# Second layer's local attention: the first pass by 64 queries and 192 keys, and TensorE tiles of 32 rows by 64 columns for both passes

## The chip, the core and the metric

The kernel runs on one core of a Trainium2 chip. The metric is the device time of one execution in microseconds; the time before is 2541.93 us, the median of three runs (2540.92, 2541.93, 2542.63). Engines are named as in the profile: PE (TensorE matmul), PEld (TensorE weight load), DVE (VectorE), ACT (ScalarE), POOL (GpSimd), SP (SyncE, whose queue issues most DMAs). L665 is line 665 of the kernel before.

## The reference, cut to what matters

Two layers run over x of shape (2, 2048, 256), in float32. Each layer normalises x, computes an attention s and a gate g, and adds s * g to x. The change is in the attention of the second layer alone. It has 16 heads of 16 channels, and a query sees the keys at most 64 positions away:

```python
def _local_mask(seq_len):
    idx = jnp.arange(seq_len)
    band = jnp.abs(idx[:, None] - idx[None, :]) <= WINDOW // 2     # WINDOW = 128
    return jnp.where(band, 0.0, -jnp.inf).astype(jnp.float32)
...
scores = jnp.einsum('bhqd,bhkd->bhqk', q, k) * SCALE + mask
attn = jax.nn.softmax(scores, axis=-1)
out = jnp.einsum('bhqk,bhkd->bhqd', attn, v)
out = out.transpose(0, 2, 1, 3).reshape(b, s, D)
return out @ w_out + b_out
```

The first layer has the same shape of attention without a mask, then a feed-forward part with low-rank experts; the second layer's feed-forward part is a linear layer with eight gated low-rank experts.

## The kernel before

**Stages.** The program is unrolled and runs: weights and first norm, the first layer's feed-forward part, its attention (about 1100 to 2125 us), the second norm with the second layer's feed-forward part and its first q and k (2125 to 2290 us), the second layer's attention (2290 to 2505 us), and a tail. One function, `attention`, serves both layers; `local=True` is the second layer.

**Layout.** Heads go in groups of four (`NG`). A group's q and k lie as [128, tokens] tiles: each head has 32 rows (`HP`), of which 16 are channels; of the other 16, k holds ones, and q holds the negated maximum of the query in the first and zeros in the rest. So a score is a matmul with 32 rows of contraction, and the four heads of a group lie on the four row groups of PE's array. `hp[j]` is the row slice of head j. In the local case k has 64 columns of padding (`PAD`) on either side.

**Items and steps.** An item is one batch element, one group of heads, and a block of 512 queries: 2 x 4 x 4 = 32 items. In the local case an item has two steps (`U` = 2), each over 256 queries, two tiles of 128. So there are 64 steps. In step s the loop calls, in this order: `scores(second, first, es)`, where `second` is step s and `first` is step s + 5 (`U + LEAD`); `weigh` for the step two back (`DEL`); and whatever `after` holds for the step.

**First pass** (in `scores`, L652 to L665): it finds each query's largest score. For each head and each of the two query tiles, one matmul takes 128 queries as the stationary operand and up to 256 keys as the moving one (`reach`, L691, cuts 64 columns off at a sequence's ends), and writes `sq`, which has a bank for each head of a pair. The pairs are (2, 3) and (0, 1); there are two `sq` buffers of two banks. DVE then adds the mask, a [128, 256] band that is the same for every tile, and takes the maximum along the keys (L672, output `seen` and a column of `mx`).

**Maximum** (`place_max`, L704 to L710): after every second step, PE transposes `mx` of a coming item into `pmx`, ACT negates it into `row`, and a DMA issued by ACT writes it into the extra row of q.

**Second pass** (in `scores`, L618 to L634): scores are computed again, with keys as the stationary operand, into `sk`, one bank per head. A bank has 512 columns: query tile 0 against key tile 0, both query tiles against key tile 1 (256 columns), and query tile 1 against key tile 2. So three matmuls per head, of 256, 128 and 128 columns, listed in `segs`. ACT takes the exponential of each bank (L681); POOL zeroes what lies outside the band, two selects for each pair of heads (L686).

**Weighing** (`weigh`, L721 to L736): 12 matmuls per step with v as the stationary operand (32 columns per head, so in tiles of 128 rows by 32 columns) accumulate into one bank `acc`; the pieces are 128, 256 and 128 columns. ACT copies 256 columns out to `av`.

**Banks.** `sk`, `acc`, `pmx` and the output projection's `pr` share the tag "m" of a pool of four PSUM banks, which they take in turn.

**Order on PE.** `scores` collects its matmuls as `pieces` with a number `when`, and issues them sorted by it. In a step with both passes (`apart`) the heads 0 and 1 of the second pass go beside the heads 2 and 3 of the first, and then the other way round, so that all four row groups have work:

```python
when = 2 * (j // 2) if apart else 0          # second pass, then += 2 * (hi - lo) / TB
when = (2, 2, 0, 0)[j] if apart else 0       # first pass, + t for the query tile
for _, o, lhs, rhs in sorted(pieces, key=lambda x_: x_[0]):
    nc.tensor.matmul(o, lhs, rhs, start=True, stop=True)
```

Each float32 matmul appears in the records as two passes, each with its own weight load.

**After an item.** The numerators and denominators go out and back by DMA (`away`, `compact`, `write`, `spread`), DVE inverts the denominators, and `divide` multiplies, on DVE and POOL in turn. After the last group of heads two output projections per item follow (L819 to L826). q and k of later groups are fetched in halves by SP.

**The mask** (L554 to L563): DVE fills a [128, 256] tile with zeros and POOL cuts the band with two selects; these instructions stand, on their engines, in the stage of the second norm, near 2133 us.

Of the kernel before, what the change touches and what calls it, by code (L numbers as in the profile page):

```python
# [10 lines left out]
F32 = mybir.dt.float32  # L11
I32 = mybir.dt.int32
AF = mybir.ActivationFunctionType
ALU = mybir.AluOpType
# [3 lines left out]
P = 128  # L18
# [7 lines left out]
TB = 512  # L26
# [4 lines left out]
MASKED = -1e30  # L31
# [6 lines left out]
def two_layers(ctx: ExitStack, tc: tile.TileContext, a, out):  # L38
    nc = tc.nc
# [444 lines left out]
    def attention(A, scale, local, final, start=None, projected=False):  # L484
# [18 lines left out]
        with ExitStack() as st:  # L503
# [43 lines left out]
            hp = [slice(j * HP, (j + 1) * HP) for j in range(NG)]  # L547
            ep = None if local else pool("ep", 8)
# [3 lines left out]
            if local:  # L552

                mask = mp.tile([P, 2 * P], F32, name="mask", bufs=1)  # L554
                nc.vector.memset(mask, 0.0)
                nc.gpsimd.affine_select(
                    out=mask, in_=mask, compare_op=ALU.is_ge, fill=MASKED, base=0,
# [3 lines left out]
                    out=mask, in_=mask, compare_op=ALU.is_ge, fill=MASKED, base=P,  # L561
                    pattern=[[-1, 2 * P]], channel_multiplier=1,
                )  # L563

# [29 lines left out]
            def scores(second, first, es):  # L594
# [7 lines left out]
                if second:  # L602
# [3 lines left out]
                    if local:  # L606

                        qt = n * TT + 2 * u
                        segs = [
                            (P, 3 * P, bass.ts(qt + 1, P), bass.ds(qt * P, 2 * P)),  # L610
                            (0, P, bass.ts(qt, P), bass.ts(qt, P)),
                            (3 * P, 4 * P, bass.ts(qt + 2, P), bass.ts(qt + 1, P)),
                        ]
                    else:
                        segs = [(0, TB, bass.ts(u, P), bass.ts(n, TB))]
# [8 lines left out]
                    for j in range(NG):  # L624
# [6 lines left out]
                        when = 2 * (j // 2) if apart else 0  # L631
                        for lo, hi, ks_, qs_ in segs:
                            pieces.append((when, t[:, lo:hi], k[hp[j], ks_], q[hp[j], qs_]))
                            when += 2 * (hi - lo) / TB  # L634
                        tasks.append((es[j], t))
                pairs = []
                if first:
# [9 lines left out]
                    for pair in ((2, 3), (0, 1)):  # L647
                        sq = pmax.tile([P, 2, TB], F32, name="sq", tag="sq")
                        pairs.append((pair, sq))
                        for d, j in enumerate(pair):  # L650
                            when = (2, 2, 0, 0)[j] if apart else 0
                            if local:  # L652
                                for t in range(2):
                                    qt, lo, hi = reach(n1, u1, t)
                                    pieces.append((
                                        when + t, sq[:, d, t * 2 * P + lo : t * 2 * P + hi],
                                        q1[hp[j], bass.ts(qt, P)], k1[hp[j], qt * P + lo : qt * P + hi],
                                    ))
# [7 lines left out]
                for pair, sq in pairs:  # L666
                    if local:
                        for d, j in enumerate(pair):
                            for t in range(2):
                                qt, lo, hi = reach(n1, u1, t)  # L670
                                seen = mp.tile([P, 2 * P], F32, name="seen", tag="seen")
# [498 lines left out]
```

## Time and profile before

| what | value |
|---|---|
| median of three runs | 2541.93 us (2540.92 to 2542.63) |
| the profiled execution, own time | 2539.57 us |
| its span on the core | 2537.7 us |
| granted PE clock over the span | 0.999 |
| second layer's attention, 2290 to 2505 us: PE, DVE, ACT, POOL busy | 213.2, 182.8, 149.9, 175.1 of 215 us |
| second norm and feed-forward part, 2125 to 2290 us: PE, DVE, ACT, POOL busy | 163.4, 59.3, 57.5, 10.9 of 165 us |
| first layer's attention, 1100 to 2125 us: PE, DVE busy | 1021.8, 804.5 of 1025 us |

The times come from one profiled execution, in which each instruction has a start and a length. The ends of matmuls are modelled, so "busy" on PE is an upper view. In a group's line the first part names line, engine and operation, then output and inputs by the program's names, their shapes and how many there were; behind the bar stand the busy time in us, the mean of one in ns, and the idle time of the engine just before them with what ended it. A timeline line merges neighbouring instructions of the same kind: start, length of the merged piece, and after the x the number of instructions. Matmuls in different tiles of the array overlap, so their lengths don't add up; the distance from start to start tells the pace.

### The profile page before, as it was taken

What the parts mean: (1) busy time and instruction counts of PE and PEld (TensorE: products, weight loads), DVE (VectorE), ACT (ScalarE), POOL (GpSimd) and SP (SyncE); (2) the same over time, 40 slices, a digit from 0 to 9 for tenths busy, and PEclk for the clock granted to TensorE, in tenths of its full rate; (3) what the DMA queues carried; (4) which work ended last, traced back from release to release, by engine and by line L of the source; (5) the groups of instructions that cost most, each with busy time, mean ns of one, the idle gap of its engine ahead of it and who ended that gap; (6) DMA issues with size and microseconds to landing.
All of it is one profiled execution on the core that took longest, in us unless ns stands there. A gap on an engine that the chain in (4) does not pass through costs nothing.

```text
span 2537.7 us, 47965 instructions
## 1 busy us (share of the span) xinstructions
PE 2514.2 (99%) x18928; PEld 1062.5 (42%) x18928; DVE 1686.9 (66%) x2744; ACT 1625.0 (64%) x3190; POOL 879.6 (35%) x830
## 2 busy tenths in 40 slices
PE   8999999999999999999999999999999999999999
PEld 5444444543333333333333333333333334457766
DVE  4143333157888888888777788888888765238986
ACT  5300000127888888888888888888888886227755
POOL 0000000102344444444444444444444430016887
PEclk9999999999999999999999999999999999999999
DMA  6131111330001001001001001001000002133552
GB/s 243 51 88 51 52 51 34 113 86 14 16 12 43 16 12 43 17 12 48 12 12 43 16 13 43 16 12 43 16 12 10 16 12 61 50 133 107 167 161 83
DMA packets 80689, 129.56 MB, mean 51 GB/s; under 512 B 27408, under 2 KB 32400, under 8 KB 77904
## 3 DMA queue, kind: packets, MB, share of 16 engines
q1 hardware_dynamic: 78592, 125.20, 15.7%
q8 instruction: 148, 2.42, 0.4%
q10 hardware_dynamic: 1872, 1.31, 0.2%
q14 instruction: 77, 0.63, 0.1%
HBM read 80.24 MB, written 45.70 MB: 50 GB/s over the span
## 4 chain that ended last, share of the span: by engine, by line
PE 80%; DVE 0%; ACT 0%; issue 0%; POOL 0%; ACTq 0%; POOLq 0%; DVEq 0%
PE sk L665 25%; PE acc L731 23%; PE sq L665 19%; PE pp L477 4%; PE pr L819 2%; PE pp L530 2%; PE po L1007 1%; PE pt L1003 1%; PE po L1015 1%; PE pmx L704 0%; PE xb L138 0%; PE xb L113 0%; DVE part L677 0%; PE of L811 0%; PE pw L990 0%
## 5 line engine op out<-in xcount | busy, mean ns | idle before, releaser
L677 DVE TENSOR_REDUCE part<-sq 128x2 f32<-128x1024 f32 x1024 | 1207.3, 1221 | 301.6 <-PE sq L665 301.2
L681 ACT ACTIVATE e<-sk 128x512 f32<-128x512 f32 x2048 | 1058.3, 603 | 222.7 <-PE sq L665 194.2
L665 PE MATMUL sk<-q,k 32*128 32x512 f32 (+2 forms) x5632 | 1141.6, 533 | 1.4 <-ACT xn L681 1.0
L665 PE MATMUL sq<-k,q 32*128 32x512 f32 (+2 forms) x5120 | 1129.5, 569 | 1.3 <-DVE part L677 1.3
L745 POOL TENSOR_TENSOR av<-av,more 128x512 f32<-128x512 f32 x462 | 585.0, 1266 | 941.1 <-ACT more L744 941.1
L665 PEld LDWEIGHTS sk<-q,k 32*128 32x128 f32 x5632 | 523.2, 184 | 579.8 <-ACT e L681 482.9
L731 PE MATMUL acc<-e,v 128*32 128x512 f32 x4096 | 546.4, 605 | 0.0
L665 PEld LDWEIGHTS sq<-k,q 32*128 32x128 f32 x5120 | 407.5, 183 | 23.7 <-DVE part L677 12.2
L744 ACT COPY more<-acc 128x512 f32<-128x512 f32 x462 | 270.4, 585 | 1.0 <-issue 0.5
L731 PEld LDWEIGHTS acc<-e,v 128*32 128x32 f32 x4096 | 81.5, 108 | 388.3 <-ACT e L681 378.4
L461 ACT ACTIVATE gt<-po 128x512 f32<-128x512 f32 x16 | 8.8, 594 | 321.1 <-PE po L457 321.1
L672 DVE CUSTOM_DVE_ANT_0 seen<-sq,mask 128x256 f32<-128x256 f32 (+1 forms) x512 | 176.2, 410 | 52.7 <-PE sq L665 46.3
L467 POOL TENSOR_TENSOR x<-x,up 128x512 f32<-128x512 f32 x16 | 23.1, 1461 | 446.5 <-DVE up L464 446.5
L448 DVE TENSOR_TENSOR xs<-we,px 128x512 f32<-128x512 f32 x64 | 44.0, 687 | 136.1 <-PE px L440 131.8
L686 POOL TENSOR_SCALAR_AFFINE_SELECT xn<-xn 128x512 f32<-128x512 f32 x172 | 105.9, 649 | 77.8 <-ACT xn L681 74.0
L440 PE MATMUL px<-xn,FV 128*128 128x512 f32 x256 | 121.2, 595 | 0.0
L444 PE MATMUL py<-cum,FW 128*128 128x512 f32 x256 | 120.5, 593 | 0.6 <-DVE cum L412 0.6
L424 PE MATMUL po<-pr,UO 128*128 128x512 f32 x256 | 119.0, 592 | 0.0
L681 ACT ACTIVATE xn<-sk 128x512 f32<-128x512 f32 x172 | 89.9, 601 | 40.6 <-PE sk L665 17.9
L450 DVE TENSOR_TENSOR pr<-xs,py 128x512 f32<-128x512 f32 x64 | 44.0, 688 | 64.9 <-PE py L444 64.6
L424 PEld LDWEIGHTS po<-pr,UO 128*128 128x128 f32 x256 | 48.6, 190 | 61.2 <-issue 61.0
L444 PEld LDWEIGHTS py<-cum,FW 128*128 128x128 f32 x256 | 48.4, 190 | 61.5 <-issue 59.8
(195 smaller groups left out, 1608.0 us busy)
## 6 DMA issues: line engine op xcount, KB each, us to landing
we<-wd SPq DMA_DIRECT2D x128, 128.0 KB
ad<-av SPq DMA_DIRECT2D x59, 256.0 KB
qd<-sb SPq DMA_DIRECT2D x48, 256.0 KB
k<-qd SPq DMA_DIRECT2D x10, 1024.0 KB
q<-qd SPq DMA_DIRECT2D x10, 1024.0 KB
xn<-ad SPq DMA_DIRECT2D x59, 128.0 KB
recb<-rd SPq DMA_DIRECT2D x59, 128.0 KB
q<-qd SPq DMA_DIRECT2D x12, 512.0 KB
```

What stands on the lines that cost most here:

```text
L424: nc.tensor.matmul(po[oc], UO[:, ch, bass.ts(oc, P)], pr, start=(ch == 0), stop=False)
L440: nc.tensor.matmul(px, FV[:, c, bass.ts(ch, P)], xn[b][:, c, cols], start=(c == 0), stop=(c == NC - 1))
L444: nc.tensor.matmul(py, FW[:, c, bass.ts(ch, P)], cum[:, c, :], start=(c == 0), stop=(c == NC - 1))
L477: nc.tensor.matmul(ps, w[:, c, bass.ts(hf, P)], xn[b][:, c, bass.ts(n, TB)], start=(c == 0), stop=(c == NC - 1))
L665: nc.tensor.matmul(o, lhs, rhs, start=True, stop=True)
L672: nc.vector.tensor_tensor_reduce(seen[:, lo:hi], sq[:, d, t * 2 * P + lo : t * 2 * P + hi], mask[:, lo:hi], 1.0, LOWEST, ALU.add, ALU.max, ...
L677: nc.vector.tensor_reduce(pt[:, pair[0] : pair[1] + 1, t, kb], sq, AX.X, ALU.max)
L681: nc.scalar.activation(e, t, AF.Exp, scale=scale)
L686: nc.gpsimd.affine_select(out=e[:, :, c, :], in_=e[:, :, c, :], compare_op=ALU.is_ge, fill=0.0, base=0, pattern=[[0, 4], [sign, P]], chann ...
L731: nc.tensor.matmul(acc[hp[j], o : o + hi - lo], vs[b][:, kt, vcols(g, j)], es[j][:, lo:hi], start=(r == 0), stop=(r == len(parts) - 1), sk ...
L744: nc.scalar.copy(more, acc)
L745: nc.gpsimd.tensor_tensor(avs[i], avs[i], more, ALU.add)
```

## The change

The first pass is cut into tiles of 64 queries, each against the 192 keys that its queries can reach: `RC` is 192, and the two halves of a query tile (`halves`) write partitions 0 to 63 and 64 to 127 of `sq`. Where one matmul had 128 stationary and up to 256 moving columns, two now have 64 and 192 each. The reduction on DVE reads 192 columns instead of 256. Since the two halves start at keys that are 64 apart, the mask is shifted by 64 for the lower half; at a sequence's first and last tile the padding columns are masked, so there are three masks of [128, 192], made of the old band (now `reach`) by six copies and two fills on DVE. The function `reach` is gone.

The second pass keeps its columns, but takes the keys in two halves of 64, each writing its half of the partitions of `sk`. So both passes use tiles of 32 rows and 64 columns. The numbers `when` are set to the new lengths. Per step the first pass issues 16 matmuls instead of 8 and the second 24 instead of 12. The first layer issues what it did before.

```diff
--- before.py
+++ after.py
@@ -545,22 +545,32 @@
 
             mp, op = pool("mp", 2), pool("op", 1)
             hp = [slice(j * HP, (j + 1) * HP) for j in range(NG)]
+            halves = [slice(sub * P // 2, (sub + 1) * P // 2) for sub in range(2)]
+            RC = P + 2 * PAD // 2
             ep = None if local else pool("ep", 8)
 
 
             pmax, pm = pool("pmax", 2, space=PSUM), pool("pexp", 4, space=PSUM)
             if local:
 
-                mask = mp.tile([P, 2 * P], F32, name="mask", bufs=1)
-                nc.vector.memset(mask, 0.0)
+
+                reach = mp.tile([P, 2 * P], F32, name="reach", bufs=1)
+                nc.vector.memset(reach, 0.0)
                 nc.gpsimd.affine_select(
-                    out=mask, in_=mask, compare_op=ALU.is_ge, fill=MASKED, base=0,
+                    out=reach, in_=reach, compare_op=ALU.is_ge, fill=MASKED, base=0,
                     pattern=[[1, 2 * P]], channel_multiplier=-1,
                 )
                 nc.gpsimd.affine_select(
-                    out=mask, in_=mask, compare_op=ALU.is_ge, fill=MASKED, base=P,
+                    out=reach, in_=reach, compare_op=ALU.is_ge, fill=MASKED, base=P,
                     pattern=[[-1, 2 * P]], channel_multiplier=1,
                 )
+
+                mask = mp.tile([P, 3, RC], F32, name="mask", bufs=1)
+                for m in range(3):
+                    for sub, p in enumerate(halves):
+                        nc.vector.tensor_copy(mask[p, m, :], reach[p, sub * PAD : sub * PAD + RC])
+                nc.vector.memset(mask[halves[0], 1, :PAD], MASKED)
+                nc.vector.memset(mask[halves[1], 2, RC - PAD :], MASKED)
 
                 efirst = xn[1].rearrange("p c t -> p (c t)").rearrange("p (i s c f) -> p i s c f", i=4, c=2, f=P)
                 elast = op.tile([P, 2, 4, 2, P], F32, name="elast")
@@ -605,14 +615,17 @@
                     q, k, _ = tiles(i)
                     if local:
 
+
                         qt = n * TT + 2 * u
                         segs = [
-                            (P, 3 * P, bass.ts(qt + 1, P), bass.ds(qt * P, 2 * P)),
-                            (0, P, bass.ts(qt, P), bass.ts(qt, P)),
-                            (3 * P, 4 * P, bass.ts(qt + 2, P), bass.ts(qt + 1, P)),
+                            (sub, lo, hi, bass.ds((qt + kt) * P + sub * PAD, PAD), bass.ds(q0, hi - lo))
+                            for kt, lo, hi, q0 in (
+                                (1, P, 3 * P, qt * P), (0, 0, P, qt * P), (2, 3 * P, 4 * P, (qt + 1) * P)
+                            )
+                            for sub in range(2)
                         ]
                     else:
-                        segs = [(0, TB, bass.ts(u, P), bass.ts(n, TB))]
+                        segs = [(None, 0, TB, bass.ts(u, P), bass.ts(n, TB))]
                     if local:
                         slots = [exponentials() for _ in range(2)]
                         for j in range(NG):
@@ -628,10 +641,11 @@
                             t = spare[:, j - 2]
                         else:
                             t = pm.tile([P, TB], F32, name="sk", tag="m")
-                        when = 2 * (j // 2) if apart else 0
-                        for lo, hi, ks_, qs_ in segs:
-                            pieces.append((when, t[:, lo:hi], k[hp[j], ks_], q[hp[j], qs_]))
-                            when += 2 * (hi - lo) / TB
+                        when = [1.5 * (j // 2) if apart and local else 2 * (j // 2) if apart else 0] * 2
+                        for sub, lo, hi, ks_, qs_ in segs:
+                            o = t[:, lo:hi] if sub is None else t[halves[sub], lo:hi]
+                            pieces.append((when[sub or 0], o, k[hp[j], ks_], q[hp[j], qs_]))
+                            when[sub or 0] += 2 * (hi - lo) / TB
                         tasks.append((es[j], t))
                 pairs = []
                 if first:
@@ -651,11 +665,12 @@
                             when = (2, 2, 0, 0)[j] if apart else 0
                             if local:
                                 for t in range(2):
-                                    qt, lo, hi = reach(n1, u1, t)
-                                    pieces.append((
-                                        when + t, sq[:, d, t * 2 * P + lo : t * 2 * P + hi],
-                                        q1[hp[j], bass.ts(qt, P)], k1[hp[j], qt * P + lo : qt * P + hi],
-                                    ))
+                                    for sub in range(2):
+                                        q0 = (n1 * TT + 2 * u1 + t) * P + sub * PAD
+                                        pieces.append((
+                                            when + t * RC / (2 * P), sq[halves[sub], d, bass.ts(t, RC)],
+                                            q1[hp[j], bass.ds(q0, PAD)], k1[hp[j], bass.ds(q0, RC)],
+                                        ))
                             else:
                                 t, kb = divmod(u1, NB)
                                 pieces.append((
@@ -667,10 +682,10 @@
                     if local:
                         for d, j in enumerate(pair):
                             for t in range(2):
-                                qt, lo, hi = reach(n1, u1, t)
-                                seen = mp.tile([P, 2 * P], F32, name="seen", tag="seen")
+                                qt = n1 * TT + 2 * u1 + t
+                                seen = mp.tile([P, RC], F32, name="seen", tag="seen")
                                 nc.vector.tensor_tensor_reduce(
-                                    seen[:, lo:hi], sq[:, d, t * 2 * P + lo : t * 2 * P + hi], mask[:, lo:hi],
+                                    seen, sq[:, d, bass.ts(t, RC)], mask[:, (qt == 0) + 2 * (qt == NT - 1), :],
                                     1.0, LOWEST, ALU.add, ALU.max, mx[:, j, 2 * u1 + t : 2 * u1 + t + 1],
                                 )
                     else:
@@ -687,11 +702,6 @@
                                 out=e[:, :, c, :], in_=e[:, :, c, :], compare_op=ALU.is_ge, fill=0.0, base=0,
                                 pattern=[[0, 4], [sign, P]], channel_multiplier=-sign,
                             )
-
-            def reach(n, u, t):
-
-                qt = n * TT + 2 * u + t
-                return qt, (PAD if qt == 0 else 0), (2 * P - PAD if qt == NT - 1 else 2 * P)
 
             pin = tc.keep_in_program_order
 
```

## The prediction

> **What bounds the kernel now.** I read the page first, then the second layer's attention by itself: windows, groups by shape, and the timelines of PE and ACT over two steps. The page says PE is the engine of the whole program:
>
> ```profile
> PE 2514.2 (99%) x18928; PEld 1062.5 (42%) x18928; DVE 1686.9 (66%) x2744; ACT 1625.0 (64%) x3190; POOL 879.6 (35%) x830
> ```
>
> That share does not price an edit to one stage. The windows (columns: length, PE, PEld, DVE, ACT, POOL busy, granted clock, DMA share, GB/s) show the stage itself:
>
> ```profile
> 2350.00:2375.00 25.00, 24.94 (x500) 19.97 (x496) 22.99 (x129) 18.31 (x43) 21.97 (x34) 1.00 0.52 152
> 2375.00:2400.00 25.00, 24.94 (x496) 19.47 (x494) 23.16 (x129) 18.98 (x44) 21.35 (x33) 1.00 0.57 164
> ```
>
> DVE (23 of 25) and POOL (22 of 25) are nearly as full as PE, whose ends are modelled. So four engines pace each other here. The stage's groups, from 2250 to 2400 us:
>
> ```profile
> L672 DVE CUSTOM_DVE_ANT_0 seen<-sq,mask 128x256 f32<-128x256 f32 x267 | 96.5, 419 | 37.5 <-PE sq L665 32.9 <-PE sk L665 4.5 <-issue 0.2
> L665 PE MATMUL sq<-k,q 32*128 32x256 f32 x540 | 68.7, 394 | 0.0
> L665 PE MATMUL sk<-q,k 32*128 32x128 f32 x528 | 43.5, 270 | 0.0
> L672 DVE CUSTOM_DVE_ANT_0 seen<-sq,mask 128x192 f32<-128x192 f32 x36 | 12.6, 353 | 9.2 <-PE sq L665 9.2
> ```
>
> The 192-wide reduction, today only at a sequence's ends, takes 353 ns against 419; start to start in the DVE timeline it is 0.278 against 0.344 us. Now two steps on PE, then on ACT (columns: start, length):
>
> ```profile
> 2347.14 0.48 PE L665 MATMUL sk<-q,k 32*128 32x256 f32 x2
> ...
> 2348.95 0.38 PE L665 MATMUL sq<-k,q 32*128 32x256 f32 x2
> 2349.26 1.08 PE L731 MATMUL acc<-xn,v 128*32 128x128 f32 x24
> 2350.26 0.28 PE L704 MATMUL pmx<-ident,mx 128*16 128x128 f32 x1
> 2350.47 0.62 PE L665 MATMUL sk<-q,k 32*128 32x256 f32 x2
> 2350.62 0.48 PE L665 MATMUL sq<-k,q 32*128 32x256 f32 x2
> ...
> 2352.25 0.28 PE L665 MATMUL sk<-q,k 32*128 32x128 f32 x2
> 2352.54 1.08 PE L731 MATMUL acc<-xn,v 128*32 128x128 f32 x24
> ```
>
> ```profile
> 2348.44 2.12 ACT L681 ACTIVATE elast<-sk 128x512 f32<-128x512 f32 x4 [0.71 <-POOL xn L686]
> 2350.45 0.38 ACT L736 COPY av<-acc 128x256 f32<-128x256 f32 x1
> 2350.70 0.26 ACT L707 ACTIVATE row<-pmx 16x128 f32<-16x128 f32 x1
> 2350.99 0.53 ACTq L710 DMA_DIRECT2D q<-row  x1
> 2351.80 2.06 ACT L681 ACTIVATE xn<-sk 128x512 f32<-128x512 f32 x4 [0.84 <-PE sk L665]
> ```
>
> A step is a scores stretch (first sk to first acc), then acc, 1.006 us to whatever follows it, and in every second step pmx, 0.207. The plain stretch here took 2.11, the one after pmx 2.07. What ends them? The four banks of tag "m" rotate through sk0 to sk3 and acc, so **acc may not start until the first exponential has emptied sk0's bank**. In the second step that exponential starts at 2351.80, lasts 0.60, and acc follows 0.14 after its end; most steps after pmx show the same 0.143. In the plain step acc starts 0.31 after the last sq matmul, which is PE's own pace (0.21 of stream, 0.09 of change of tiling), but the exponential had ended only 0.22 before. So removing PE work uncovers this chain: sk0 done, first exponential, acc.
>
> From the starts in the PE timeline: 25 stretches after pmx sum to 54.3 us (mean 2.17), 24 plain ones to 52.5 (median 2.11; four of 2.33 to 2.39 and one of 2.98, where sq of heads 0 and 1 came late behind DVE), 8 between output projections to 16.0, and the two steps before the first acc took 5.5 together.
>
> **The change, part by part.** *First pass.* Per step and head, two matmuls of 256 columns on a 128-wide tile become, on each of two 64-wide tiles, two of 192. Each is two passes in the records; a 256-column pass repeats every 0.2155 us, so columns cost 0.83 ns each plus about 2.5 ns, and 192 give 0.1625. Per row group 4 x 0.053 = 0.21 us less, if both halves stream at once.
>
> *Second pass.* Same 512 columns per tile, 64 keys wide instead of 128: no column saved. The first weights of a stretch lie open: passes 1 and 2 start 0.32 apart, not 0.2155, so 0.105 for 128 columns; on acc, 32 columns, that excess is 0.025. I take 0.052 for 64, a gain of 0.05.
>
> *PE alone* would then need 0.05 (weights), 0.87 (sk), 0.65 (sq) and 0.09 (change of tiling): 1.66 us, against its own best of 1.95 now.
>
> *The exponential's chain.* In the plain step sk0's last pass starts 0.87 into the stretch and the first exponential 1.30; the change moves only the weights' 0.05, giving 1.244. Plus 0.597 plus 0.143: acc at **1.984**, later than PE's 1.66. After pmx, ACT also waits for the last sq of heads 2 and 3, issued before sk0's end; these wait behind sk1, whose bank the fourth exponential frees late (sk1 0.14 late above). That exponential ends 3.35 after the plain stretch's start and the next begins at 3.20, so sk1 slips 0.21; with 192 columns sq still ends at 1.08, level with sk0. I take 1.99.
>
> *DVE.* Eight reductions of 0.278 instead of 0.344 save 0.53 us a step, so the late stretches should fall to the plain value; ACT's calls in two steps add to about 5.8 us of 6.19, just free in time. POOL's four selects (0.587 each, 2.35) and its 1.26 division every fourth step fit into 4 x 3.1. An exponential needs its slot three steps later, so POOL hides; without that slack each 0.1 us lost there is 6 us in all.
>
> *Masks.* Six 64x192 copies and two small fills, on DVE between the statistics of the second norm, near 2134 to 2138. Nearest rows: the 128x256 fill there took 0.27, a 128x2 operation 0.16; so 8 x 0.17 = 1.4 us at most. DVE idles 1.5 us there ahead of the reciprocal, and PE has projections to run. Behind them wait only those statistics. Between 0 and 1.4, I take 0.5. POOL's two selects stay. No DMA is added; the scheduler swaps a few q and k transfers on SP, which I price at 0, with 0.5 us either way.
>
> Sum, us: after pmx 25 x 1.99 = 49.8, so -4.5; plain 24 x 1.984 = 47.6, so -4.9; with projections 4 x 1.98 + 4 x 1.90 = 15.5, so -0.5 (the plain four there lack 0.08 of semaphore handling); the two steps before acc become DVE's 16 x 0.278 = 4.45, so -1.0; five stretches of first pass alone, 0.26 each, -1.3; five of second pass alone, 0.05 each, -0.25; masks +0.5. Together **-12.0**. The span 2537.7 becomes 2525.7, the profiled run 2539.57 becomes 2527.6. The median of the runs, 2541.93, stands 2.4 above the profiled run; so 2530.
>
> Ends: if narrow weights gain nothing and sk1 still delays the exponential, the stretches are 2.04 and 2.17 and 6 us are lost, with masks 7: 2537. If the chain gives way by half of the 0.3 us that PE has left, 57 x 0.15 more: 2521.
>
> **A rule against this change.** The change doubles PE's score instructions: 80 weight loads and 80 matmuls per stretch for 40 and 40, 210 a step with acc and pmx. The rows: between two semaphore records of PE's sequencer, 2349.126 and 2349.573, stand acc's 48 instructions, so 9.3 ns each; the densest whole steps bound it from above, 130 in 3.08 us, 23.7. I take 9.3, the only row in which the sequencer itself is timed: 1.95 us a step, hidden under 3.1; at 23.7 a step would be 4.98 and the kernel 110 us slower.
> [...]
>
> **The rivals.** *One half at a time (slower).* If two 64-wide tiles on the same rows share one stream, a stretch's PE time is 0.05 + 2 x 0.87 + 2 x 0.65 + 0.09 = 3.18, 1.0 more than now, in 59 steps: about 2600. It decides once a pass is stretched 1.3 times, since 1.66 x 1.3 = 2.16. For it: the trace has no two tiles on the same rows and different halves. Against it: acc's four 32-wide tiles start 7 ns apart on the same rows, and four row groups do in the scores. Either row alone says concurrent; whether they compose is unseen.
> [...]
>
> *The sequencer (slower).* Above 14.8 ns an instruction the scores are decoded too late for 2.04 us stretches; at 18, 0.6 us a step: 2575.
>
> *Nothing to see.* The stage swings around another engine: POOL at 22 of 25 us, or ACT, whose last call before the next exponential leaves only 0.06. Then only DVE's late stretches and the first-only steps gain, 3 to 4 us: 2538.
>
> *More than forecast.* If acc does not wait for the first exponential, PE's 1.66 rules (POOL's 2.75 a step below it): 57 x 0.32 = 18 more, at best 2512.
>
> **How the numbers follow.** Forecast 0.60 (its own range 2521 to 2537), more 0.08, nothing 0.11 (2537 to 2547), half at a time 0.12, sequencer 0.09. The range 2515 to 2552 holds the forecast, most of "more" and all of "nothing", some 0.78, and the small slowdowns add a little. About 0.2% (5.1 us) is what a measurement can tell from no change: faster 0.68, same 0.12, slower 0.20. The predicted time is 2530.
>
> **What would show it.** Right: sq and sk in 32x64 shapes with starts 7 ns apart; seen at 0.28 start to start; DVE below 20 of 25; both kinds of stretch near 1.98, with acc 0.14 after the first exponential's end and PE idle ahead of it. Wrong: sq passes of one row group alternating between halves; stretches above 2.2; sk weights waiting on "issue"; or acc starting right after the last matmul.

## The result and the profile after

The changed kernel takes 2559.68 us, the median of four runs (2551.82 to 2561.02), against 2542.19 us of the kernel before (four runs, 2540.92 to 2542.63). The ratio is 1.0062, with a 95% interval of 1.005 to 1.0074: slower by 0.6%, outside the predicted range of 2515 to 2552. The profiled run took 2560.09 us, its span 2558.4 us.

The span divides at two events that both traces have, the last `acc` of the first layer and the first `sq` of the second:

| us | before | after | difference |
|---|---|---|---|
| up to the last `acc` of the first layer | 2110.57 | 2113.65 | +3.1 |
| from there to the first `sq` of the second layer | 139.24 | 140.38 | +1.1 |
| from there to the end (the stage) | 287.9 | 304.3 | +16.4 |

The first row is no part of the change. The difference is there by the 200th matmul (50.56 us against 47.48) and then stays. Of the sixteen kernels run later, which all have the same instructions there, five reach that `acc` as early as the kernel before (within 0.3 us), ten come 2.5 to 3.5 us later and one 5.5. In the early ones PE's granted clock is at full speed up to that `acc`; in each of the late ones, and in the changed kernel, it is 0.50 for 3.41 us near 20 us and, in some, again near 470 us. So the stage is compared by its own length below.

In the page's first part and its list of queues, two lines answer:

```profile
PE 2514.9 (98%) x21488; PEld 1056.4 (41%) x21488; DVE 1660.4 (65%) x2752; ACT 1626.2 (64%) x3190; POOL 880.0 (34%) x830
q8 instruction: 168, 2.75, 0.5%
```

PE has 2560 matmuls and 2560 weight loads more. The instruction queue q8 moved 148 packets of 16 KB before and moves 168 now: 20 more, and 5120 / 20 is 256 records for each packet, that is 64 bytes a record. These packets are PE's instructions, in pages.

The windows of the two stretches of time shown before (length, PE, PEld, DVE, ACT, POOL busy, granted clock, DMA share, GB/s):

```profile
2350.00:2375.00 25.00, 19.94 (x626) 14.54 (x610) 15.65 (x100) 14.60 (x33) 17.48 (x27) 0.93 0.52 159
2375.00:2400.00 25.00, 23.18 (x772) 17.45 (x765) 18.16 (x118) 17.59 (x40) 20.48 (x31) 1.00 0.44 129
```

Where PE was busy for 24.94 of 25 us it now stands still for 5 us in the first window and 1.8 in the second. (The granted clock of 0.93 in the first is taken up with the stage's sum below.) DVE fell below 20, as forecast, but ACT and POOL fell too: no engine took over as the bound. The groups from 2250 to 2400 us, by shape:

```profile
L687 DVE CUSTOM_DVE_ANT_0 seen<-sq,mask 128x192 f32<-128x192 f32 x272 | 78.8, 353 | 67.5 <-PE sq L680 61.8 <-PE sk L680 5.7
L680 PE MATMUL sq<-k,q 32*64 32x192 f32 x1104 | 59.3, 335 | 4.8 <-issue 4.8
L680 PEld LDWEIGHTS sk<-q,k 32*64 32x64 f32 x1409 | 44.7, 131 | 12.1 <-issue 5.9 <-ACT xn L696 3.1 <-ACT elast L696 1.0
```

The shapes are the intended ones, and the reduction takes the forecast's 353 ns. New is "issue" as a releaser of `sq` and `sk`: PE waited there for nothing that the profile shows. The waits of PE from 2297 us to the end (total, times, longest) put them together:

```profile
PE sq L680 <- issue: 8.0, 6, 2.7
PE acc L741 <- issue: 4.4, 3, 2.7
PE sk L680 <- issue: 4.1, 5, 1.3
```

One of them, in the timeline of PEld:

```profile
2401.41 0.69 PEld L741 LDWEIGHTS acc<-xn,v 128*32 128x32 f32 x14
2405.07 0.14 PEld L741 LDWEIGHTS acc<-xn,v 128*32 128x32 f32 x2 [2.97 <-issue]
2405.41 0.09 PEld L714 LDWEIGHTS pmx<-ident,mx 128*16 128x16 f32 x1 [0.20 <-issue]
```

The stall lies inside `acc`, between two of its 24 passes, where the profile shows no semaphore that PE waits for. Counting PE's records (weight loads, matmuls, semaphore events) from the program's start, every long stall of the stage falls on an index that leaves 193 when divided by 256. From the first `acc` on there are 51 such places; 23 of them have a gap above 0.15 us, together 23.4 us. Up to the last 15 us of the program, the gaps at any other remainder sum to 2.6 us at most, and in the kernel before no remainder reaches 1.8. (A gap is counted here from the start of the record before it. From the modelled end of PE's last matmul to the next, the same places come to 16.5 us.)

Most of these gaps can be worked out, 17 of the 23 within 0.1 us. After such a place (a crossing, from one page to the next), the next packet on q8 starts some time later, takes about 1 us, and where PE has been waiting it resumes about 1.33 us after the packet's end. If that round trip is longer than PE takes for the page it is working on, the rest is the gap (from the trace's records; us):

```
next crossing   packet starts after + takes + 1.33 = round trip   page at full pace   rest    gap seen
2313.81               3.17          1.02             5.52               3.53         1.99     1.90
2326.68               2.27          1.01             4.61               3.53         1.08     1.08
2361.25               1.23          1.01             3.57               4.16         none     0.00
2371.85               4.33          0.95             6.61               3.53         3.08     3.11
2405.07               4.58          1.01             6.92               4.03         2.89     2.98
```

The median round trip is 3.9 us, a tenth are above 5.5. A page lasts 3.5 to 4.2 us at the new pace (210 records in a step of some 3.05 us) and lasted 6.2 to 6.7 us before (130 in 3.25): its fetch was hidden.

Between the stalls the forecast's mechanism is there. PE, then ACT, in a plain step:

```profile
2362.76 0.32 PE L680 MATMUL sk<-q,k 32*64 32x128 f32 x4
2363.17 1.08 PE L741 MATMUL acc<-elast,v 128*32 128x128 f32 x24
```

```profile
2362.43 2.07 ACT L696 ACTIVATE xn<-sk 128x512 f32<-128x512 f32 x4 [0.62 <-PE sk L680]
```

The last `sk` pass starts at 2362.76, `acc` 0.41 later: it waits. The first exponential runs from 2362.43 for 0.60, and `acc` starts 0.14 after its end. Of the 57 stretches, 25 took 1.94 to 1.99, ten 2.04 to 2.06, one 1.88, and 21 more than that.

### The profile page after: what moved, and what is told of

Same layout as the page of the kernel before. It is cut to its first block, busy times and chain, and to the rows that moved or that the text cites. A ratio compares the mean times of both kernels' runs of the same rounds, so it can differ in the third digit from the quotient of the medians.

```text
span 2558.4 us, 53104 instructions
## 1 busy us (share of the span) xinstructions
PE 2514.9 (98%) x21488; PEld 1056.4 (41%) x21488; DVE 1660.4 (65%) x2752; ACT 1626.2 (64%) x3190; POOL 880.0 (34%) x830
## 4 chain that ended last, share of the span: by engine, by line
PE 79%; issue 1%; DVE 1%; ACT 1%; POOL 0%; DMA 0%; ACTq 0%; SPq 0%; DVEq 0%; POOLq 0%
PE sk L680 24%; PE acc L741 22%; PE sq L680 19%; PE pp L477 4%; PE pr L829 2%; PE pp L530 2%; PE po L1017 1%; PE pt L1013 1%; PE po L1025 1%; PE pmx L714 0%; PE xb L138 0%; PE xb L113 0%; DVE part L692 0%; PE of L821 0%; DMA q<-qd 0%
## 5 line engine op out<-in xcount | busy, mean ns | idle before, releaser
L680 PE MATMUL sq<-k,q 32*128 32x512 f32 (+1 forms) x6144 | 1117.8, 522 | 9.4 <-issue 8.0
L680 PEld LDWEIGHTS sk<-q,k 32*128 32x128 f32 (+1 forms) x7168 | 508.6, 161 | 585.9 <-ACT e L696 482.0
L680 PEld LDWEIGHTS sq<-k,q 32*128 32x128 f32 (+1 forms) x6144 | 392.5, 166 | 32.8 <-issue 18.3
L687 DVE CUSTOM_DVE_ANT_0 seen<-sq,mask 128x192 f32<-128x192 f32 x512 | 148.2, 353 | 91.6 <-PE sq L680 80.0
L467 POOL TENSOR_TENSOR x<-x,up 128x512 f32<-128x512 f32 x16 | 23.1, 1461 | 449.6 <-DVE up L464 277.5
L424 PEld LDWEIGHTS po<-pr,UO 128*128 128x128 f32 x256 | 48.6, 190 | 61.2 <-issue 61.2
```

Of the source, the lines that this page charges most:

```text
L424: nc.tensor.matmul(po[oc], UO[:, ch, bass.ts(oc, P)], pr, start=(ch == 0), stop=False)
L687: nc.vector.tensor_tensor_reduce(seen, sq[:, d, bass.ts(t, RC)], mask[:, (qt == 0) + 2 * (qt == NT - 1), :], 1.0, LOWEST, ALU.add, ALU.max ...
```

## The experiments

The theory, called F in the expectations: the change loses its time because PE's instruction pages are used up faster than one page can be fetched ahead. Rivals: narrow tiles cost time by themselves (C), the masks and the order around them (M), waits for data transfers (T).

**Half of the change alone.** In `half1_first_pass_only` the second pass has the old segments; in `half2_second_pass_only` the first pass, the mask and the reductions are the old ones.

```diff
 # half1, scores(): second pass
-   (sub, lo, hi, bass.ds((qt + kt) * P + sub * PAD, PAD), bass.ds(q0, hi - lo)) ...
+   (None, P, 3 * P, bass.ts(qt + 1, P), bass.ds(qt * P, 2 * P)),
+   (None, 0, P, bass.ts(qt, P), bass.ts(qt, P)),
+   (None, 3 * P, 4 * P, bass.ts(qt + 2, P), bass.ts(qt + 1, P)),
```

> First pass in quarters and halves with 192 columns, second pass as before (128 keys wide). Per step of the second layer PE has 162 records of weight loads and matmuls instead of 210 (changed) and 130 (before). Theory F (PE waits for its instruction pages, 256 records each, only one page ahead, some 4 to 5 us from crossing to usable): a page lasts 256/162 x 3.05 = 4.8 us instead of 3.7, so the sum of PE gaps at page boundaries in the stage falls from 23.4 us to 8 or less, and the time to 2536 to 2545. Rival C (the narrow tiles or the masks themselves cost the time): mixing 64-wide and 128-wide tiles changes PE's tiling several times a stretch, at the 0.09 us seen per change stretches become 2.2 to 2.4 and the time 2555 to 2570, with the loss in every stretch and not at page boundaries.

> Second pass in 64-key halves, first pass, mask and reductions as before: no column and no reduction saved, 178 records per step. Theory F: a page lasts 256/178 x 3.2 = 4.6 us; single stalls of 0.3 to 2 us at page boundaries only, 4 to 12 us in all, time 2546 to 2555, and stretches without a boundary as before or 0.05 shorter. Rival C (narrow tiles cost by themselves): every stretch is longer than 2.17, by the same amount, 2560 or more. If F is false and narrow tiles are free: 2540 to 2544.

Measured, for the first: 2645.81 (the profiled run) and 2646.47 us, ratio 1.0406 (1.0386 to 1.0427), and in two further runs, with a granted clock of 0.942 where these had 0.998, 2784.22 and 2786.26 us. For the second: 2937.29 us, ratio 1.1542 (1.1522 to 1.1561). Both are far outside of what either theory expected. One stretch of the first, in PE's timeline:

```profile
2393.44 0.78 PE L678 MATMUL sk<-q,k 32*128 32x256 f32 x4
2394.14 0.88 PE L678 MATMUL sq<-k,q 32*64 32x192 f32 x16
2394.95 0.73 PE L678 MATMUL sk<-q,k 32*128 32x128 f32 x12
2395.61 0.55 PE L678 MATMUL sq<-k,q 32*64 32x192 f32 x8
2396.10 0.49 PE L678 MATMUL sk<-q,k 32*128 32x128 f32 x4
2396.52 0.55 PE L678 MATMUL sq<-k,q 32*64 32x192 f32 x8
2397.00 0.49 PE L678 MATMUL sk<-q,k 32*128 32x128 f32 x4
2397.42 1.08 PE L739 MATMUL acc<-xn,v 128*32 128x128 f32 x24
```

`sk` on 32x128 tiles and `sq` on 32x64 tiles come here in blocks, one after the other, although they lie on different row groups: from the start of one block to that of the next it is 0.42 to 0.81 us. In the kernel before, with one shape, `sk` and `sq` start 0.02 us apart (2347.14 and 2347.16), and so they do in the changed kernel (2405.62 and 2405.64). The stretch is 3.98 us, and 4.9 in the other kernel at full clock, where the granted clock besides fell to 0.50 to 0.54 for part of the stage (stretches of 8.66). So the two halves of the change can't be had one by one. About page stalls these runs say nothing, since their pages last longer.

**The pace of instructions alone.** `split_before` keeps the old tiles, columns and masks, and cuts each 256-column matmul in two:

```diff
-   (P, 3 * P, bass.ts(qt + 1, P), bass.ds(qt * P, 2 * P)),
+   (P, 2 * P, bass.ts(qt + 1, P), bass.ts(qt, P)),
+   (2 * P, 3 * P, bass.ts(qt + 1, P), bass.ts(qt + 1, P)),
 # first pass: for c0, c1 in ((lo, P), (P, hi)); weigh(): (0, P, 3 * P, qt + 1) in two parts likewise
```

> The kernel before with every 256-column matmul of the second layer's scores and weighting cut into two of 128 columns: same tiles, same columns, same masks and reductions, but 194 PE records per step instead of 130. Theory F: a page of 256 records lasts 4.2 us instead of 6.3; laid against the changed kernel's round trips (next fetch's start after a crossing + its length + 1.33 us; median 3.9, a tenth above 5.5) that loses about 17 us in the stage, all of it in gaps at page boundaries; with up to 2 us for the extra passes the time is 2553 to 2563. Rival C (the stalls need tiles of 64 columns of the array): no gaps at page boundaries, 2543 to 2546.

Measured: 2560.47 us, ratio 1.0078 (1.0058 to 1.0098), as slow as the changed kernel with none of its narrow tiles. PE's waits:

```profile
PE acc L733 <- issue: 7.4, 6, 2.5
PE sk L667 <- issue: 2.9, 4, 1.7
```

The gaps at one remainder of 256 sum to 14.6 us (no other above 1.9); the stage is 18.2 us longer than before. Theory F holds, a little below its 17 us; C as the cause of the stalls falls.

**What makes the round trip long.** `no_reload` and `no_reload_before` leave out the loads of q and k for the third to eighth group of heads, in the changed kernel and in the one before; so these groups are computed from other groups' data.

```diff
-                if bg >= B * NG:
+                if bg >= (2 if local else B * NG):
                     return
```

> The changed kernel without the loads of q and k for the third to eighth group of heads in the second layer's attention (they keep the first two groups' data), 12.3 MB of the 37 MB that the stage moves; all else as in the changed kernel. Theory F with contention (the page's fetch is late because its packet queues behind data on the 16 DMA engines): next fetch after a crossing begins sooner (median 1.3 us now), stalls fall from 23 to 8 to 15 us, time 2545 to 2552. Theory F without contention (the round trip belongs to the fetch itself): stalls stay at 20 to 25 us, time 2556 to 2561. Rival T (PE waits for q and k data, not for instructions): the stalls no longer lie at page boundaries and vanish with the loads, time below 2540.

> Control for no_reload: the kernel before without the loads of q and k for the third to eighth group of heads in the second layer. Theory F: its pages last over 6 us and hide their fetch already, so the loads cost it nothing and it stays at 2541 to 2544, while the changed kernel gained 20 us by the same edit. Rival T (PE waits for the loads themselves, in both kernels): it gains 10 us or more, 2532 or less.

Measured: 2539.93 us, 0.9989 of the kernel before (0.998 to 0.9998), 19.8 us below the changed kernel; the control stays, 2542.65 us, ratio 1.0002 (0.9993 to 1.0011). PE's waits in the first:

```profile
PE sq L680 <- issue: 1.6, 3, 0.8
PE sk L680 <- issue: 0.8, 1, 0.8
```

All gaps at crossings, small ones included, fall to 5.8 us (23.8 in the changed kernel); a tenth of the packets start later than 1.76 us after a crossing, where it was 3.13. The 2539.93 is below what F expected (2545 to 2552): a third of the bytes less took three quarters of the stalls. So data on the move delays the pages. In the changed kernel's trace the eight packets that started more than 2.2 us after their crossing waited while the 16 DMA engines were busy for 0.69 to 1.0 of the time (0.42 from 2297 to 2543 us). That they queue on these engines is the likely reading, though no run separates it from a slower memory. The same loads cost the kernel before nothing, and the stalls that are left still lie at crossings: theory T falls, although 2539.93 is just inside its "below 2540".

**Bursts or bytes.** Three kernels cut each pair of loads (k, then q, 1 MB) into quarters of 256 KB; in `spread_pinned` they are held in program order besides.

```diff
-                if local and n == NB // 2 - 1:
-                    at(end, fetch, b * NG + g + 2, 0, T // 2)
+                if local and n % 2:
+                    for r in range(4):
+                        lo = n // 2 * T // 2 + r % 2 * TB
+                        at(end + r, fetch, b * NG + g + 2, lo, lo + TB, (r // 2,))
```

> The changed kernel with each pair of loads (k, then q, about 1 MB back to back on SP's queue, every fourth step) cut into four of 256 KB, one a step: k, k, q, q. Same bytes, same instructions on PE. Theory F with contention: a page's fetch no longer queues behind 4 us of data, the long round trips (5.2 to 7 us) go, and of 23.4 us of stalls 8 to 14 stay; time 2543 to 2552. If bytes and not bursts set the round trip: stalls 20 to 25 us, 2556 to 2561.

> Control: the same spreading of the loads in the kernel before, whose pages hide their fetch. Both theories of the fetch: no change, 2540 to 2545. If it gains more than 5 us, the bursts cost something else than instruction pages.

> The changed kernel with the loads of q and k in quarters of 256 KB again, but now held in program order, one a step, in the order k, k, q, q (unpinned, the scheduler had put them on SP in pairs, and the write of the maxima on ACT's queue waited for some of them). Theory F with contention: the longest queue ahead of a page's fetch falls from 1 MB to 256 KB, so long round trips go and the stalls at page boundaries fall from 23.4 us to 6 to 14; time 2541 to 2553. If the row write still waits for loads, ACT stands still for it as before and the time stays above 2560 with fewer stalls at page boundaries. If bytes and not bursts set the round trip: stalls above 20 us.

Measured: 2570.56 us (ratio 1.0117, 1.0099 to 1.0134), 2555.94 us (1.0054, 1.0039 to 1.0069) and 2558.12 us (1.0065, 1.0051 to 1.0079). The stalls at crossings stay, at 27.3 us in the first and 23.1 in the third; the first has besides three waits of the kind shown below, 7.2 us. With the pinned quarters the packet still starts 1.57 us after a crossing in the median (1.49 in the changed kernel), and a tenth start after 2.69 us (3.13). Smaller bursts were no remedy. The control lost 13 us to something else, seen in ACT's timeline:

```profile
2390.13 0.26 ACT L707 ACTIVATE row<-pmx 16x128 f32<-16x128 f32 x1
2394.10 0.55 ACTq L710 DMA_DIRECT2D q<-row  x1
2394.74 2.06 ACT L681 ACTIVATE xn<-sk 128x512 f32<-128x512 f32 x4 [4.35 <-issue]
```

The DMA that writes the row of maxima, issued by ACT, was held for 3.7 us, and the exponentials stood behind it. (For two others of these waits the profile names the landing of another DMA as what ended them.) Seven such waits of 1.0 to 3.7 us sum to 13.6 us; the stage is 13.0 us longer. In the kernel before, one of 0.35 is the only one above 0.3.

**The masks alone.** `masks_unused` is the kernel before with the changed kernel's six copies and two fills, which nothing reads.

> The kernel before, with the changed kernel's six copies and two fills made and never read; reductions, matmuls and mask as before. Theory M (the mask work on DVE waits for POOL and delays the norm's statistics): +1.0 to +1.5 us between 2125 and 2230 us, time 2543 to 2544. Rival (the +1.15 us there is the order of transfers on SP, which this kernel need not change): 0 to +0.3. In both, the attention stage keeps its 287.9 us. If the first 25 us of the program are again 3 us longer, that part of the changed kernel's time is no part of the change's doing.

Measured: 2542.86 us, ratio 0.9999 (0.999 to 1.0009). Between the first layer's last `acc` and the first `sq` it takes 140.27 us for 139.24: +1.0 us, with the stage at 287.5. Theory M holds, for 1.0 us; in the median over runs it doesn't show.

**The forecast's gain without the records.** `order_before` sorts the first pass later among the second's, with no instruction added. `onepass_before` and `onepass_after` run the first pass, whose maxima cancel in the softmax, on the upper halves of q and k:

```diff
 # order_before
-   when = (2, 2, 0, 0)[j] if apart else 0
+   when = (2.6, 2.6, 0.6, 0.6)[j] if apart and local else (2, 2, 0, 0)[j] if apart else 0
 # onepass_before; the same around q1 and k1 in onepass_after
+   def high(t): return t.bitcast(mybir.dt.bfloat16).rearrange("p (f w) -> p f w", w=2)[:, :, 1]
-   q1[hp[j], bass.ts(qt, P)], k1[hp[j], qt * P + lo : qt * P + hi],
+   high(q1[hp[j], bass.ts(qt, P)]), high(k1[hp[j], qt * P + lo : qt * P + hi]),
```

> The kernel before with one number changed: the first pass's matmuls are sorted 0.6 later among the second pass's, so that both last 128-column pieces of sk0 and sk1 are issued ahead of the second half of sq for heads 2 and 3. No instruction, mask, column or record is added: 130 records per step. Theory (of the forecast: the first exponential waits in issue order for sq of heads 2 and 3 and for sk0, and ends the stretch): stretches after pmx fall from 2.17 to 2.0, as in the kernel whose matmuls were cut in two (1.997), plain ones from 2.11 to 2.0; 25 x 0.17 + 24 x 0.11 = 7 us, time 2534 to 2539, and no stalls at page boundaries. Rival: sq of heads 2 and 3 comes late for DVE instead and the gain is lost there, 2541 to 2546.

> The kernel before with the second layer's first pass (the row maxima only, subtracted again in the weights' sum) on the upper 16 bits of q and k, which are a bfloat16 value, so that each of its matmuls should be one pass instead of two: 16 of its 32 records a step go, 114 instead of 130, and half of the first pass's stream (at most 0.43 us per row group left of 0.87). Tiles, masks, reductions (256 columns), second pass as before. This is the forecast's step without its side effect: PE's own pace falls below the chain from sk0 over the first exponential to acc. Theory F: stretches of both kinds fall to 1.94 to 2.0 (from 2.11 and 2.17), a page lasts 7 us, no stalls at page boundaries; 24 x 0.13 + 25 x 0.18 = 8 us less, time 2532 to 2538. Rival N (shorter stretches are worth nothing here, POOL or DVE take over): 2541 to 2545.

> The same edit in the changed kernel: 178 records a step instead of 210, stretches as short as the chain allows (1.94, as now). Theory F: a page lasts 256/178 x 3.05 = 4.4 us instead of 3.7, stalls at page boundaries fall from 23.4 us to 8 to 15, time 2543 to 2553, that is 8 us or more behind onepass_before although its reductions are shorter and its columns fewer. Rival (the time of the changed kernel lies in its columns or tiles): as fast as onepass_before or faster.

Measured: `order_before` 2546.08 us (ratio 1.0012, 1.0003 to 1.0021), a miss. Both kinds of stretch became 2.16: the exponential starts earlier, but PE now issues until 1.855 and `acc` follows its last pass by 0.30. With two full passes of 256 columns PE's own pace is the bound.

`onepass_before` takes 2538.89 us, ratio 0.9985 (0.9976 to 0.9994), the fastest of all kernels here. The group in its trace:

```profile
L665 PE MATMUL sq<-k,q 32*128 32x256 bf16 x280 | 30.7, 278 | 0.2 <-DVE mx L672 0.2
```

The undisturbed stretches of both kinds are 1.976 to 1.980 us, the forecast's chain (1.984 and 1.99) with 114 records a step, and the gaps at no remainder exceed 2.4 us. The time is 1 us above the expected range. `onepass_after`, with 178 records, takes 2545.54 us (1.0014, 1.0006 to 1.0023): 6.7 us behind although its stretches are shorter (median 1.934). F expected the order of the two, but its stalls at crossings are 4.7 us instead of 8 to 15, and five waits of the row write, of 0.9 to 2.4 us, add 7.8 us (the expectation of the next experiment counts some of these waits twice). `onepass_before` has six, 5.0 us.

**The row write a step later.** The four kernels `late_row_...` move only this DMA, to the next step behind the copy of `acc`.

```diff
-   pin(nc.scalar.dma_start(out=q[HD:P:HP, ...], in_=row))
+   at(i * U - LEAD + 1, lambda: pin(nc.scalar.dma_start(out=q[HD:P:HP, ...], in_=row)))
```

> onepass_after with the write of the row of maxima (ACT's queue) issued one step later, behind that step's copy of acc, and a third buffer for the row. In onepass_after eight of these writes waited 0.6 to 2.9 us beyond their usual 0.54 us or less for a transfer in flight, some 10 us in all with ACT standing behind them. Theory W (this wait took the rest of the forecast's gain): it goes, the stage falls from 289.3 to 276 to 282 us and the time to 2531 to 2539. Rival (ACT's wait is hidden by its free time): 2543 to 2547, as onepass_after.

> onepass_before with the same edit. Five of its writes waited some 3.5 us in all beyond the usual. Theory W: stage from 282.6 to 278 to 281 us, time 2534 to 2538. Rival: unchanged, 2538 to 2540.

> The changed kernel with the same edit. Theory F with W: its page stalls (23.4 us) stay, since its PE records per step stay at 210; only the two writes that waited 2.7 and 2.2 us are gained, 2555 to 2560. Rival (the stalls at page boundaries come from ACT's wait): 2545 or less.

> Control: the kernel before with the same edit. It has almost no such waits outside the steps with projections: 2539 to 2544, unchanged within 0.1%.

Measured, in this order: 2547.31 us (ratio 1.0016, 1.0005 to 1.0028), 2540.88 (0.9991, 0.9983 to 1.0), 2557.39 (1.0055, 1.0042 to 1.0068) and 2549.18 (1.0028, 1.0019 to 1.0037). The control got slower by 6 us, and nothing was gained elsewhere. PE's waits in the first:

```profile
PE sk L680 <- DMA q<-row: 4.1, 5, 1.2
PE sk L680 <- issue: 3.2, 3, 1.4
```

ACT waits less for the write (four waits, 4.6 us, the longest 2.6), but the row now lands too late in five places: two steps were not enough there for this 8 KB write, and the second pass that reads it waits, 4.1 us in all. The stalls at crossings grew besides, from 4.7 to 8.2 us. So the wait moved in part from ACT to PE, and how much of the gain it holds isn't separated. The changed kernel keeps its stalls (23.6 us), which don't come from ACT.

## Why the prediction was wrong

- *The chain that bounds a stretch*: right. Forecast 1.984 and 1.99; seen 1.94 to 1.99 and 2.04 to 2.06 in the changed kernel, 1.98 for both in `onepass_before`, each with `acc` 0.14 after the first exponential's end. The 57 stretches should have lost 9.9 us. In `no_reload` they sum to 118.2 us against 122.8, with 4.9 us of stalls above 0.15 still in the stage, of which 0.4 lie in `acc`: without the rest 9.1 us less. (Five plain stretches of the kernel before, not four, took 2.33 to 2.40; the sums hold.)
- *Tiles in halves of columns*: right that they stream at once, the rival *one half at a time* (stretches of 3.18) is refuted. Not foreseen was what tiles of two shapes do: a stretch of `half1_first_pass_only` takes 3.98 us, where 1.94 to 1.99 is the chain here.
- *First-pass-only steps*: 0.836 for 1.076, 0.24 each where 0.26 was forecast.
- *The two steps before the first `acc`*: wrong. Forecast 4.45 from DVE's reductions, a gain of 1.0; seen 5.48 for 5.52. ACT, which the sum left out, sets their length: its first exponential starts 2.33 us into them, behind the row write and a table load of 1.28 us at 2296.12, and four take 2.07. DVE stands idle for 1.1 us between its two sets of eight, and PE waits 1.1 us for ACT.
- *Second-pass-only steps*: 6.2 us in all before and after, where 0.25 less was forecast.
- *Masks*: 1.0 us for 0.5, inside its 0 to 1.4.
- *The sequencer*: **the step that failed**. The prediction took 9.3 ns an instruction from a row of 48 and called 1.95 us a step "hidden under 3.1". The rate was right: over the fastest microsecond of the changed trace it is 8.9 ns. But instructions that are read at this pace must also arrive, and a row of 48 says nothing about a page of 256. The price here was not per instruction but per page: 256 records in 3.5 to 4.2 us against a round trip of 3.9 us with a long tail (a tenth above 5.5), which is 23.4 us in all and up to 3.1 at one crossing. The rival *the sequencer*, at 2575, had the right sign and about twice the loss, with the wrong mechanism and threshold: no run shows an issue pace of 14.8 or 18 ns an instruction. The text asked for "sk weights waiting on 'issue'" as its sign, and that is what came.
- *Transfers at 0*: the loads priced at nothing set how late a page comes. Without them the same kernel is 19.8 us faster.

The stage adds up: stretches +9.4 (132.2 for 122.8), `acc` +8.3 (72.7 for 64.4, with the stalls inside it), first-pass-only steps -1.1, the two steps before `acc` 0, `pmx` -0.1: +16.5 of 16.4 measured. Taking the 23.4 us of stalls away leaves a gain of 7.0 us in the stage where 12.5 were forecast. Of the difference of 5.5 us, 1.0 is the two steps before the first `acc`, and 0.5 the terms of first-pass-only and second-pass-only steps. 0.5 more is one row write near 2488 us: it waited 2.2 us, but mostly beneath a page stall of 1.5 in the same stretch, which took 4.06 where its like took 2.05. Another part shows in the granted clock (the columns as above; the clock is the third from the end):

```profile
2371.70:2375.10 3.40, 3.25 (x55) 1.93 (x55) 1.60 (x9) 1.08 (x2) 0.37 (x1) 0.51 0.32 83
2405.90:2409.30 3.40, 3.40 (x92) 3.03 (x80) 1.78 (x13) 1.69 (x4) 0.62 (x2) 0.50 0.36 105
```

These are the only two places of the stage, before its last 3 us, at half the clock, and they stand right behind its two longest stalls (3.11 and 2.98 us, ended at 2371.85 and 2405.07). In them `acc` took 1.87 and 1.29 us instead of 1.01, and the stretches beside it 0.6 and 1.0 more than others once their stalls are taken off: 2.7 us. So a long stall may cost more than its own length; that it brings the lower clock is read from the order of the two, and no run shows it by itself. Of the changed kernel's four runs the fastest, 2551.82 us, had a mean granted clock of 0.999, the others 0.996 to 0.997. Less than 1 us stays unexplained. In the other kernels the same subtraction of stalls and row waits from the stage gives 277.5 us (`no_reload`), 277.6 (`onepass_before`) and 276.8 (`onepass_after`), 10 to 11 us below the kernel before, near the forecast's 12.5; but the row wait was not removed without a new one in its place, and the clock, 0.50 for 6.8 us of the stage in `onepass_before` and for 13.7 in `onepass_after`, is not in it. So that part is argued, not shown.

## What to carry to other kernels

When a change doubles the instructions of an engine, divide the records of a page by the records per microsecond, and lay the time that the page lasts against the round trip of its fetch. Here PE used up a page of 256 records in 3.5 to 4.2 us, the round trip was 3.9 us in the median and above 5.5 for a tenth of the pages, with the DMA engines busy for 0.42 of the time (from 2297 to 2543 us), and PE stood still for 23.4 us at page boundaries, which the profile puts down to "issue" in places that share nothing but their index; in the kernel before, at 6.2 to 6.7 us a page, the gaps at no remainder reached 1.8. Look at the tile shapes of the matmuls in flight together: with two of them the stretch took 3.98 us, with one 1.94 or 2.11. And a DMA issued by a busy engine can become a wait on that engine: in `spread_before` seven waits of ACT for its row write, the longest 3.7 us, came with a stage 13.0 us longer, where the kernel before has none above 0.35.

## What the runs showed that had not been expected

- PE's instructions came in packets of 16 KB for 256 records; where PE stood still, it resumed 1.2 to 1.6 us after the packet's end in 21 of 23 gaps (the others 0.76 and 3.39).
- In `half1_first_pass_only` matmuls on 32x128 and 32x64 tiles on different row groups came in blocks, one after the other: 3.98 us for a stretch that takes 2.11 with one shape and 1.94 with the other. In `half2_second_pass_only`, with `sk` narrow and `sq` wide, the granted clock fell to 0.50 (from 2480 to 2530 us).
- The start of the program takes one of three lengths (47.2 to 47.5, 48.3 to 48.6 or 50.6 to 51.3 us to the 200th matmul) in kernels that don't differ there. The first shows the full granted clock, the second 0.50 for 3.41 us from about 18 us, the third the same from about 20 us.
